# An attention and Mamba kernel whose small TensorE work is handed out at about one matmul a block

## The chip, the cores and the metric

The kernel runs on one core of one Trainium2 chip. The metric is the device time of one execution in microseconds (us). The engines are TensorE (PE, with its weight loads PEld), VectorE (DVE), ScalarE (ACT), GpSimd (POOL) and SyncE (SP), which issues most DMAs.

## The reference

Two layers act on x of shape (4, 128, 64, 64), all in fp32. Layer 0 is self-attention over the 4096 pixels of each image, with 4 heads of 32 channels, followed by a residual and a layer norm over channels. Layer 1 is the sum of three branches on the result: a 3x3 convolution, a spectral branch (a 2-D FFT, a 1x1 product over real and imaginary parts, the inverse FFT), and a Mamba block. Cut to what matters:

```python
attn = softmax(q @ k.T * scale); y = layernorm(attn @ v @ Wo + bo + x) * gamma + beta   # layer 0
spatial = conv3x3(y, conv_spatial_w) + conv_spatial_b
spectral = irfft2(conv1x1(rfft2(y)))
xi, z = split(u @ in_proj_w.T)                      # u: y as (pixels, 128); 256 channels each
xs = silu(conv1d_causal(xi, 4 taps))
dt = softplus(xs @ x_proj -> 8 -> dt_proj + b);  B, C = xs @ x_proj -> 16 + 16
h[t] = exp(dt[t] * A) * h[t-1] + dt[t] * B[t] * xs[t]     # 256 channels x 16 states
ym = ((sum over states of h * C) + xs * D) * silu(z) @ out_proj_w.T
out = spatial + spectral + ym
```

## The kernel before

**Blocks.** An image is cut into 8 chunks of 512 pixels; there are 32 chunks. Attention handles a chunk in two units, one per pair of heads (H = 0 to 63), each against all 4096 keys. The program is one long Python loop over *blocks* (`u`), and every engine executes its instructions in the order in which this loop records them. One unit takes 16 blocks, one chunk 32 (`SLOT`). A block during attention holds, on PE in this order:

- `scores_for_max` (L444), four matmuls into a two-bank PSUM tile (tag sA) for a coming unit; DVE takes the row maxima of it (L451);
- two times `scores_for_exp` (L486), six matmuls each, the first into tag sB, the second into tag sC; ACT takes exp of each (L494);
- a second `scores_for_max` with its L451, again in sA, of which there is one buffer;
- other PE work, see below;
- two times `times_values` (L506), exp times V into tag o.

The eight PSUM banks are sA, sB and sC with two each, m and o with one each.

**The scan.** 64 blocks (`LAG = 2 * SLOT`) behind attention, each block also does one of a chunk's 32 scan steps (16 states, two halves of channels): ACT writes the decay exp(dt A) to PSUM in one half of a tile with tag sC (`scan_decay`, L771), DVE runs the scan (`scan_state`, L784), POOL multiplies with C (L788) and adds to the sum (L803), and prepares dt B xs two steps ahead (`scan_input_term`, L776). For the last two chunks PE sums instead (L797), and after attention has ended DVE does L776.

**Other work.** Everything else is a set of generators that `Plan` drives: K and V projections (`project_kv`, L365 and L378), queries (`project_q`, L423), the transposes of maxima (`maxima`, L457, L466, L473), the output projection with layer norm (L562, L563, bn_stats L571, L589), the inputs of the Mamba block (`mamba_input` L639, `scan_input` L663 with the causal taps L670/L675 on DVE), `scan_bc` (L696), `scan_dt` (L707 to L737), `gate` (L746), `spectral` (L813, L820, L821), `convolve` (nine matmuls L840 and one L844) and `scan_output` (L894). A generator yields a string of what its next step needs: P a place for a matmul, C one of the convolution, T a temporary PSUM bank, A a place on ACT, D, E and g on DVE at three points of the block, M the lasting bank, x and f buffers. Each block has so many places of each kind, and the jobs take them by rank and by due time (`plan.at(u, rank, job)`). The temporaries of a block are the two banks of one tile `tmp` with tag sB, made when the first is asked for:

```python
t = psum.tile([P, 2, L], F32, tag="sB", name=f"tmp_{u}")
return [t[:, 0, :], t[:, 1, :]]
...
places = {"P": 2, "C": 1, "T": 2, "A": 3, "D": 2, "E": 1, "G": 1}
```

`sigmoid` is built of exp and ln, since one table set holds both: Abs, Exp and Ln(1 + .) on ACT, one DVE instruction at point g, after the scan (L611), which reads the logarithm, and Exp again (L613). The logarithm (L609) takes a temporary bank of its own. Each chunk has four sigmoids, two of the taps' output and two of the gate. `scan_dt` has a logarithm of the same kind, twice a chunk (L724, read by L727).

Of the kernel before, what the change touches and what calls it, by code (L numbers as in the profile page):

```python
# [9 lines left out]
F32 = mybir.dt.float32  # L10
# [7 lines left out]
P = 128  # L18
# [5 lines left out]
L = 512  # L24
# [57 lines left out]
class Job:  # L82
# [3 lines left out]

    def __init__(self, gen, u):  # L90
        self.gen = gen
        self.done = False
# [11 lines left out]
class Plan:  # L104


    def __init__(self, temporary, lasting, buffers):
        self.u = None
        self.places = {}
        self.buffers = buffers  # L110
        self.temporary, self.lasting = temporary, lasting
        self.seq = 0
        self.later = []
        self.jobs = []
        self.freed = []
# [11 lines left out]

    def begin(self, u, places):
        self.u = u
        self.places = dict(places)  # L130
        self.temps = []
        self.buffers["M"] += sum(when <= u for when in self.freed)
        self.freed = [when for when in self.freed if when > u]

    def phase(self, kinds):
        u = self.u
        for e in sorted((e for e in self.later if e[0] <= u), key=lambda e: e[:3]):
            self.jobs.append((e[1], e[0], e[2], Job(e[3], u - 1)))
            self.later.remove(e)
        self.jobs = sorted((j for j in self.jobs if not j[3].done), key=lambda j: j[:3])  # L140
        for *_, job in self.jobs:
            while not job.done and self.may(job, kinds):
                bank = None
                for c in job.need:
                    if c == "T":
                        if not self.temps:
                            self.temps = self.temporary(u)
                        bank = self.temps.pop(0)
                    elif c == "M":
                        bank = self.lasting(u)  # L150
                    if c in self.buffers:
                        self.buffers[c] -= 1
                    elif c != "g":
                        self.places[c] -= 1
                job.advance(bank, u)
        self.jobs = [j for j in self.jobs if not j[3].done]
# [14 lines left out]
def attention_then_conv_mamba(  # L171
# [19 lines left out]
    B, C, N = x.shape  # L191
# [144 lines left out]
    rows = [slice(j * HS, (j + 1) * HS) for j in range(2)]  # L336
    used = [slice(j * HS, j * HS + HD + 1) for j in range(2)]

    def temporary(u):

        t = psum.tile([P, 2, L], F32, tag="sB", name=f"tmp_{u}")
        return [t[:, 0, :], t[:, 1, :]]

    def lasting(u):
        return psum.tile([P, L], F32, tag="m", name=f"sum_{u}")

    plan = Plan(temporary, lasting, {"x": 2, "f": 1, "M": 1})


    def load_x(c, tag, bufs):  # L350
# [250 lines left out]
    def sigmoid(z, tag, nm):  # L601

        a = loc.tile([P, L], F32, tag=tag, name=f"sg_{nm}", bufs=1)
        yield "A"
        nc.scalar.activation(a, z, AF.Abs)
        yield "A"
        nc.scalar.activation(a, a, AF.Exp, scale=-1.0)
        ln = yield "ATG"
        nc.scalar.activation(ln, a, AF.Ln, bias=ones)  # L609
        yield "g"  # L610
        nc.vector.scalar_tensor_tensor(a, z, 0.0, ln, ALU.min, ALU.subtract)  # L611
        yield "A"
        nc.scalar.activation(a, a, AF.Exp)  # L613
        return a
# [90 lines left out]
    def scan_dt(c, hf, xd):  # L705
        pdt = yield "PTA"
        nc.tensor.matmul(  # L707
            pdt, dtw[:, hf * P : (hf + 1) * P], xd[:DTR, :], start=True, stop=True
        )


        z = loc.tile([P, L], F32, tag=f"dt{hf}", name=f"dt_{c}_{hf}")
        nc.scalar.activation(z, pdt, AF.Identity, bias=col("dt_b", hf))
        e = loc.tile([P, L], F32, tag=f"sg{hf}", name=f"spe_{c}_{hf}", bufs=1)
        yield "A"
        nc.scalar.activation(e, z, AF.Abs)
        yield "A"
        nc.scalar.activation(e, e, AF.Exp, scale=-1.0)
        yield "A"
        u = loc.tile([P, L], F32, tag=f"u{hf}", name=f"u_{c}_{hf}")  # L720
        w = u
        nc.scalar.activation(w, e, AF.Identity, bias=ones)
        ln = yield "AATG"
        nc.scalar.activation(ln, w, AF.Ln)  # L724
        nc.scalar.activation(w, w, AF.Identity, bias=minus_one)
        yield "g"
        nc.vector.scalar_tensor_tensor(z, z, 0.0, ln, ALU.max, ALU.add)  # L727
        nc.gpsimd.tensor_tensor(e, w, e, ALU.subtract)
        nc.gpsimd.tensor_tensor(z, z, e, ALU.subtract)
        nc.gpsimd.tensor_tensor(u, z, xss[c][hf], ALU.mult)  # L730
        dts[c][hf] = z
        us[c][hf] = u

        for _ in range(2):
            yield ""
        yield "A"
        nc.scalar.activation(xss[c][hf], xss[c][hf], AF.Copy, scale=col("D", hf))  # L737
        scaled.add((c, hf))
# [23 lines left out]
    def scan_decay(c, v):  # L762
        n, hf = divmod(v, NH)
        k = hf * NS + n


        if plan.u > UNITS and v % 2:
            dA[c, v] = psum.tile([P, L], F32, tag="o", name=f"dA_{c}_{k}")
        else:
            dA[c, v] = psum.tile([P, 2, L], F32, tag="sC", name=f"dA_{c}_{k}")[:, 0, :]  # L770
        nc.scalar.activation(dA[c, v], dts[c][hf], AF.Exp, scale=negA[:, k : k + 1])  # L771

    def scan_input_term(c, v, engine):
# [55 lines left out]
    def convolve(c):  # L829

        i = c % NCH
        while c not in edges or c not in hxs:
            yield ""
        flat = yield "PMC"
        pf = flat.rearrange("p (r w) -> p r w", w=W)
        for k in range(9):
            if k:
                yield "PC"
            dy, dx = divmod(k, 3)
            nc.tensor.matmul(  # L840
                pf, cw[:, k, :], xps[c][:, dy : dy + RPC, dx : dx + W], start=k == 0, stop=False
            )
        yield "PCA"
        nc.tensor.matmul(flat, g_hil, hxs.pop(c), start=False, stop=True)  # L844
        plan.release()
        ym = loc.tile([P, L], F32, tag="ym", name=f"ym_{c}", bufs=2)
        yms[c] = ym
        nc.scalar.activation(ym, flat, AF.Identity, bias=col("conv_b"))
        if i == 0:
            nc.gpsimd.tensor_tensor(ym[:, :W], ym[:, :W], sbias, ALU.add)  # L850
# [20 lines left out]
    def scan_output(c):  # L871

        b, i = divmod(c, NCH)
        late = i < NCH // 2
        yield "f"
        while not all(gates[c]):
            yield ""

        for hf in range(NH):
            if c >= CHUNKS - 2:  # L880
                acc = loc.tile([P, L], F32, tag=f"acc{hf}", name=f"acc_{c}_{hf}")
                nc.vector.tensor_tensor(acc, accs[c, hf], gates[c][hf], ALU.mult)
                accs[c, hf] = acc
            else:
                nc.gpsimd.tensor_tensor(accs[c, hf], accs[c, hf], gates[c][hf], ALU.mult)
        if not late:
            wr = load_flipped(c)
        yield ""
        yield ""
        while c not in yms:  # L890
            yield ""
        pf = yield "PPTE"
        for hf in range(NH):
            nc.tensor.matmul(  # L894
                pf, outw[:, hf, :], accs[c, hf], start=hf == 0, stop=hf == NH - 1
            )
        ob = loc.tile([P, L], F32, tag="ob", name=f"ob_{c}", bufs=1)
        nc.vector.tensor_tensor(ob, yms.pop(c), pf, ALU.add)
        if late:
            yield ""  # L900
            ymd[c] = dram.tile([P, L], F32, tag="ymd", name=f"ymd_{c}", bufs=NCH)
            nc.sync.dma_start(ymd[c], ob)
        else:
            add_flipped(ob, wr)
            yield ""
            yield ""
            nc.sync.dma_start(out[b, :, i * L : (i + 1) * L], ob)
        plan.buffers["f"] += 1
# [22 lines left out]
    UH = NT // 2  # L931
    SLOT = PAIRS * UH
    UNITS = HALVES * UH
    LAG = 2 * SLOT
    STATES = NH * NS
    for b in range(B):


        u0 = (b * NCH - 1) * SLOT + 2
        for i in range(NCH):  # L940
            plan.at((b - 1) * NCH * SLOT + i * SLOT + 20 if b else 3 - SLOT + i, 0, project_kv(b, i))
            for k in range(PAIRS):
                plan.at(u0 + k * UH + 2 * i, 0, place_k(b, k, i))
            plan.at(u0 + UH + 2 * i, 0, place_v(b, i))
# [8 lines left out]
    for c in range(CHUNKS):  # L953
# [2 lines left out]
        plan.at(u0 + 8, 1, mamba_input(c))  # L956
        plan.at(u0 + SLOT + 19, 3, convolve(c))
        plan.at(c * SLOT + LAG + 5, 3, gate(c))
        plan.at((c + 1) * SLOT + LAG, 0, scan_output(c))
    for b in range(B):  # L960
        for i in range(NCH // 2):
            plan.at((b + 1) * NCH * SLOT + 22 + 5 * i, 4, flips(b * NCH + NCH // 2 - 1 - i))
# [4 lines left out]

            scores_for_max(h + 1, s, "sC" if h < 0 and s % 2 else "sA")

    places = {"P": 2, "C": 1, "T": 2, "A": 3, "D": 2, "E": 1, "G": 1}  # L970
    most = {"P": 4, "C": 4, "T": 2, "A": 4, "D": 4, "E": 4, "G": 4}
    u = 3 - SLOT
    end = (CHUNKS + 3) * SLOT
    while u < end or not plan.idle():
# [14 lines left out]
        n = v // NH + 2  # L989
        if v % NH == 0 and 0 <= n < CHUNKS * NS:  # L990
            scan_load(*divmod(n, NS))
        plan.phase(["P", "C", "T", "A", "E", "G", "M", "x", "f", ""])
        if scan:
            scan_state(*divmod(v, STATES))
        if 0 <= v + 2 < CHUNKS * STATES:
# [83 lines left out]
```

## Time and profile before

| | |
|---|---|
| median of 3 runs | 6483.5 us (6479.47 to 6487.86) |
| the profiled execution's own time | 6482.18 us |
| its span, first to last instruction | 6480.4 us |
| granted clock of TensorE, mean | 0.983 |
| busy: PE, DVE, ACT, POOL | 5923.2, 4457.2, 3688.8, 4632.6 us |
| last attention block ends at about | 6211 us |

A line such as `L451 DVE TENSOR_REDUCE part<-s` names the source line, the engine, the operation, what is written and what is read. "A <- B" in the table of waits means that A stood idle until B was done. Matmul busy times overlap each other, since matmuls are pipelined.

### The profile page before, as it was taken

The numbers are of one execution on the slowest core, as the hardware profiler recorded it, in microseconds if no ns is written. First come the engines' busy times: TensorE is split into PE (matmuls) and PEld (weight loads), VectorE is DVE, ScalarE is ACT, GpSimd is POOL, SyncE is SP. The second block draws the span as 40 slices with busy tenths as digits, with TensorE's granted clock in tenths as the row PEclk, the third lists the DMA queues.
The fourth block names the chain that finished last, engine by engine and source line by source line (L and its number), as shares of the span: only waits on it lengthen the run. The fifth ranks groups of instructions, "written<-read, shape, count | busy, mean of one in ns | idle before, by whom it ended". The sixth has DMA issues, their size and how long they took to land.

```text
span 6480.4 us, 84221 instructions
## 1 busy us (share of the span) xinstructions
PE 5923.2 (91%) x32076; PEld 2624.0 (40%) x32076; DVE 4457.2 (69%) x4396; ACT 3688.8 (57%) x4922; POOL 4632.6 (71%) x4960
## 2 busy tenths in 40 slices
PE   5999999999999999999999999999999999999976
PEld 2444444444444444444444444444444444444421
DVE  3557777677776777777777777767777777777645
ACT  1456565566555656556556656555655665666642
POOL 0017777777787777777787777777778777777866
PEclk8999999999999999999999999999999999999976
DMA  3002222223222222222322221222322222212223
GB/s 107 14 26 56 60 54 61 60 61 90 71 71 61 61 61 53 60 58 71 89 78 63 58 61 53 61 60 63 89 66 70 56 56 56 50 52 56 58 61 88
DMA packets 234229, 405.01 MB, mean 62 GB/s; under 512 B 38872, under 2 KB 40416, under 8 KB 233824
## 3 DMA queue, kind: packets, MB, share of 16 engines
q1 hardware_dynamic: 229440, 397.75, 23.8%
q8 instruction: 251, 4.11, 0.3%
q10 hardware_dynamic: 4384, 1.89, 0.1%
q14 instruction: 154, 1.26, 0.1%
HBM read 350.54 MB, written 49.02 MB: 62 GB/s over the span
## 4 chain that ended last, share of the span: by engine, by line
PE 65%; ACT 14%; DVE 9%; POOL 4%; issue 4%; DMA 3%; SPq 0%; ACTq 0%; POOLq 0%; DVEq 0%
PE po L506 21%; PE s L486 15%; PE s L444 15%; ACT e L494 7%; DVE part L451 4%; PE sum L840 4%; ACT dA L771 3%; POOL hs L788 2%; DMA xk<-in_x 2%; DVE hs L784 2%; DVE xh L589 1%; PE tmp L562 1%; PE tmp L707 1%; ACT tmp L609 1%; PE tmp L894 1%
## 5 line engine op out<-in xcount | busy, mean ns | idle before, releaser
L451 DVE TENSOR_REDUCE part<-s 128x2 f32<-128x1024 f32 x2048 | 2502.0, 1223 | 1455.3 <-PE s L444 1450.3
L494 ACT ACTIVATE e<-s 128x1024 f32<-128x1024 f32 x2048 | 1986.9, 1022 | 2217.2 <-PE s L486 2217.2
L506 PE MATMUL po<-e,V 128*33 128x512 f32 x8192 | 1986.6, 599 | 1.4 <-ACT e L494 1.2
L444 PE MATMUL s<-K,Q 64*128 64x512 f32 x8192 | 1501.0, 445 | 101.7 <-DVE part L451 95.9
L784 DVE TENSOR_TENSOR_SCAN hs<-dA,state,db 128x512 f32<-128x512 f32 x1024 | 1310.8, 1280 | 279.4 <-ACT dA L771 220.5
L486 PE MATMUL s<-Q,K 64*128 64x512 f32 x8192 | 1302.1, 395 | 171.8 <-DVE sg_x L611 92.3
L788 POOL TENSOR_TENSOR hs<-hs,bc 128x512 f32<-128x512 f32 x1024 | 1313.7, 1283 | 81.9
L776 POOL TENSOR_TENSOR db<-u,bc 128x512 f32<-128x512 f32 x963 | 1231.4, 1279 | 0.0
L803 POOL TENSOR_TENSOR acc<-acc,hs 128x512 f32<-128x512 f32 x900 | 1154.8, 1283 | 70.6
L444 PEld LDWEIGHTS s<-K,Q 64*128 64x128 f32 x8192 | 621.5, 186 | 1320.1 <-DVE part L451 811.4
L787 POOL COPY state<-hs 128x1 f32<-128x1 f32 x1024 | 216.2, 211 | 1022.4 <-DVE hs L784 1019.5
L486 PEld LDWEIGHTS s<-Q,K 64*128 64x128 f32 x8192 | 750.8, 184 | 428.4 <-DVE sg_x L611 113.6
L506 PEld LDWEIGHTS po<-e,V 128*33 128x33 f32 x8192 | 389.4, 109 | 1194.4 <-issue 594.3
L486 PE MATMUL s<-MX,sel 64*128 64x512 f32 x4096 | 807.6, 390 | 0.0
L771 ACT ACTIVATE dA<-dt,negA 128x512 f32<-128x512 f32 x1024 | 707.5, 691 | 126.5 <-DVE hs L784 95.1
L486 PEld LDWEIGHTS s<-MX,sel 64*128 64x128 f32 x4096 | 385.3, 184 | 88.1
L840 PE MATMUL sum<-xp,cw 128*128 128x512 f32 x576 | 318.6, 638 | 0.0
L797 PE MATMUL acc<-hs,cst 128*128 128x512 f32 x128 | 112.7, 988 | 89.5 <-POOL hs L788 89.4
L460 POOL COPY wide<-mx 128x128 f32<-128x128 f32 x256 | 63.7, 295 | 154.9 <-DVE mx L457 90.2
L685 POOL TENSOR_TENSOR xs<-xs,sg_x 128x512 f32<-128x512 f32 x64 | 82.1, 1282 | 111.2 <-ACT sg_x L613 111.2
L840 PEld LDWEIGHTS sum<-xp,cw 128*128 128x128 f32 x576 | 91.9, 192 | 129.7 <-issue 129.7
L538 POOL TENSOR_TENSOR oz<-oz,rz 128x512 f32<-128x512 f32 x64 | 81.3, 1270 | 87.4 <-DMA rz<-rd 79.5
(189 smaller groups left out, 3652.4 us busy)
## 6 DMA issues: line engine op xcount, KB each, us to landing
bc<-bcd SPq DMA_DIRECT2D x512, 512.0 KB
K<-kd SPq DMA_DIRECT2D x64, 256.0 KB
rz<-rd SPq DMA_DIRECT2D x128, 128.0 KB
vd<-vst SPq DMA_DIRECT2D x32, 264.0 KB
V<-vd SPq DMA_DIRECT2D x32, 264.0 KB
xq<-in_x SPq DMA_DIRECT2D x32, 256.0 KB
xk<-in_x SPq DMA_DIRECT2D x32, 256.0 KB
kd<-khi SPq DMA_DIRECT2D x32, 256.0 KB
```

The costliest lines, as they stand in the source:

```text
L444: nc.tensor.matmul(sc[:, j, :], QT[H][rows[j], n, t * P : (t + 1) * P], KK[k][m][rows[j], :], start=n == 0, stop=n == 1,)
L451: nc.vector.tensor_reduce(part[H][:, t, :, m], sc, AX.X, ALU.max)
L486: nc.tensor.matmul(s[:, j, :], sel[rows[j], :] if n == 2 else KK[k][i][rows[j], t * P : (t + 1) * P], mov[rows[j], :], start=n == 0, stop= ...
L494: nc.scalar.activation(e, s, AF.Exp)
L506: nc.tensor.matmul(po[H][used[j], :], VA[i][:, t, 2 * k + j, :], e[:, j, :], start=m == 0, stop=m == NT - 1,)
L771: nc.scalar.activation(dA[c, v], dts[c][hf], AF.Exp, scale=negA[:, k : k + 1])
L776: engine.tensor_tensor(db[c, v], us[c][hf], bcs[c, n][:, 0, :], ALU.mult)
L784: nc.vector.tensor_tensor_scan(hs, dA.pop((c, v)), db.pop((c, v)), state[:, k : k + 1], ALU.mult, ALU.add)
L787: nc.gpsimd.tensor_copy(state[:, k : k + 1], hs[:, L - 1 :])
L788: nc.gpsimd.tensor_tensor(hs, hs, bcs[c, n][:, 1, :], ALU.mult)
L803: nc.gpsimd.tensor_tensor(accs[c, hf], accs[c, hf], hs, ALU.add)
L840: nc.tensor.matmul(pf, cw[:, k, :], xps[c][:, dy : dy + RPC, dx : dx + W], start=k == 0, stop=False)
```

## The change

Four things are changed in the code.

1. *Places.* P falls from 2 to 1.2 a block, and what is left over (up to 1) is carried into the next block. A job that needs more P than there is sets one aside for the next block. The kind C is dropped, so the convolution competes for P alone.
2. *Temporaries.* There is one T a block, the first bank of a tile `first` with tag sB (outside attention there may be two). The logarithms of `sigmoid` and `scan_dt` ask for the new kind U instead of T: the second bank of a tile `second` with tag sC, whose first bank holds the block's decay.
3. *Times and ranks.* `LAG` is 8 blocks more; K and V projections of later images may start 24 blocks earlier and have rank 2 instead of 0; `scan_output` has rank 2 instead of 0.
4. *scan_output* asks for the buffer f after its products with the gate instead of before them.

```diff
@@ class Plan
-    def __init__(self, temporary, lasting, buffers):
+    def __init__(self, banks, buffers):
...
+        self.kept = 0
...
     def begin(self, u, places):
         self.u = u
+        left = self.places.get("P", 0) + self.kept
+        self.kept = 0
         self.places = dict(places)
-        self.temps = []
+        self.places["P"] += min(left, 1)
...
         for *_, job in self.jobs:
+            if "P" in kinds and job.need.count("P") > self.places["P"]:
+                self.places["P"] -= 1
+                self.kept += 1
             while not job.done and self.may(job, kinds):
                 bank = None
                 for c in job.need:
-                    if c == "T":
-                        if not self.temps:
-                            self.temps = self.temporary(u)
-                        bank = self.temps.pop(0)
-                    elif c == "M":
-                        bank = self.lasting(u)
+                    if c in self.banks:
+                        bank = self.banks[c](u)
@@ temporaries
     def temporary(u):
-        t = psum.tile([P, 2, L], F32, tag="sB", name=f"tmp_{u}")
-        return [t[:, 0, :], t[:, 1, :]]
+        if u not in first:
+            first[u] = [psum.tile([P, 2, L], F32, tag="sB", name=f"first_{u}"), 0]
+        first[u][1] += 1
+        return first[u][0][:, first[u][1] - 1, :]
+
+    def banks_of_second(u):
+        if u not in second:
+            second[u] = psum.tile([P, 2, L], F32, tag="sC", name=f"second_{u}")
+        return second[u]
+
+    def beside_decay(u):
+        return banks_of_second(u)[:, 1, :]
...
-    plan = Plan(temporary, lasting, {"x": 2, "f": 1, "M": 1})
+    plan = Plan({"T": temporary, "U": beside_decay, "M": lasting}, {"x": 2, "f": 1, "M": 1})
@@ sigmoid
-        ln = yield "ATG"
+        ln = yield "AUG"
@@ scan_dt
-        ln = yield "AATG"
+        ln = yield "AAUG"
@@ scan_decay
-            dA[c, v] = psum.tile([P, 2, L], F32, tag="sC", name=f"dA_{c}_{k}")[:, 0, :]
+            dA[c, v] = banks_of_second(plan.u)[:, 0, :]
@@ convolve
-        flat = yield "PMC"
+        flat = yield "PM"
...
-                yield "PC"
+                yield "P"
...
-        yield "PCA"
+        yield "PA"
@@ scan_output
-        yield "f"
         while not all(gates[c]):
             yield ""
...
+        yield "f"
         if not late:
             wr = load_flipped(c)
@@ times, ranks, places
-    LAG = 2 * SLOT
+    LAG = 2 * SLOT + 8
...
-            plan.at((b - 1) * NCH * SLOT + i * SLOT + 20 if b else 3 - SLOT + i, 0, project_kv(b, i))
+            plan.at((b - 1) * NCH * SLOT + i * SLOT - 4 if b else 3 - SLOT + i, 2 if b else 0, project_kv(b, i))
...
-        plan.at((c + 1) * SLOT + LAG, 0, scan_output(c))
+        plan.at((c + 1) * SLOT + LAG, 2, scan_output(c))
...
-    places = {"P": 2, "C": 1, "T": 2, "A": 3, "D": 2, "E": 1, "G": 1}
-    most = {"P": 4, "C": 4, "T": 2, "A": 4, "D": 4, "E": 4, "G": 4}
+    places = {"P": 1.2, "T": 1, "U": 1, "A": 3, "D": 2, "E": 1, "G": 1}
+    most = {"P": 4, "T": 2, "U": 1, "A": 4, "D": 4, "E": 4, "G": 4}
...
-        plan.phase(["P", "C", "T", "A", "E", "G", "M", "x", "f", ""])
+        plan.phase(["P", "T", "U", "A", "E", "G", "M", "x", "f", ""])
```

## The prediction

> **What bounds the kernel now.** I read the page first: TensorE (PE) is busy 91% of the span, no other engine over 71%. The window view of one chunk in mid-run, of a late chunk and of the tail comes next (columns: length; busy time and count of PE, weight loads, DVE, ACT, POOL; granted clock; DMA share; GB/s).
>
> ```profile
> PE 5923.2 (91%) x32076; PEld 2624.0 (40%) x32076; DVE 4457.2 (69%) x4396; ACT 3688.8 (57%) x4922; POOL 4632.6 (71%) x4960
> ```
>
> ```profile
> 3001.84:3194.46 192.62, 180.27 (x1001) 80.35 (x1000) 137.76 (x136) 115.25 (x154) 148.90 (x159) 1.00 0.35 90
> 5088.97:5278.22 189.25, 177.86 (x990) 79.08 (x988) 136.75 (x135) 114.06 (x153) 149.04 (x159) 1.00 0.21 55
> ...
> 6211.00:6361.80 150.80, 93.38 (x148) 32.39 (x148) 85.85 (x97) 48.92 (x84) 87.25 (x96) 0.67 0.33 79
> 6361.80:6465.00 103.20, 66.35 (x88) 20.64 (x88) 58.46 (x61) 26.45 (x40) 61.15 (x67) 0.67 0.34 89
> ```
>
> A chunk of 32 blocks repeats every 192.62 us (6.02 a block), and PE has about 12 us of gaps in it. Timing each block from its first L444 matmul to the next block's, a block with no other PE work lasts 4.56 us wherever nothing is late, one with one 128x512 matmul pair-pass (L840, L746, L844) 5.62: 1.06 a matmul. All other PE work of a chunk, costed so (21 such pieces 22.3; two output projections 3.06; the L894, L696 and L820/821 products 5.66; three sets of transposes 1.77), makes 32.8 us, so 145.9 + 32.8 = 178.7 us is stall-free and 13.9 us a chunk is stall. The table of waits (engine and line, what it waited for: us in total, times, longest) says of what:
>
> ```profile
> ACT e L494 <- PE s L486: 2217.2, 1030, 12.2
> ...
> PE s L486 <- DVE sg_x L611: 92.3, 62, 2.4
> ...
> PE s L486 <- DVE sg_z L611: 71.6, 60, 1.5
> ...
> PE tmp L663 <- ACT mhi L471: 39.1, 31, 1.4
> ...
> PE tmp L813 <- ACT xi L666: 29.3, 31, 1.1
> ...
> PE tmp L746 <- ACT Q L426: 27.1, 29, 1.0
> ...
> PE tmp L423 <- ACT vst L388: 19.6, 24, 0.8
> ```
>
> ACT's 2217 us of waiting for PE confirms the bound; it costs nothing. PE itself waits in two ways. First, two temporaries in one block share one tile `tmp`: the second matmul waits for ACT to read the first. Second, after a block with the sigmoid's logarithm (L609, in `tmp`), the first exponent scores of the next block (L486, same tag sB) wait for DVE's L611, which reads that logarithm. One block of each, from the timeline (start, length):
>
> ```profile
> 3004.59 1.13 PE L423 MATMUL tmp<-xq,wq_t 128*128 128x512 f32 x2
> ...
> 3005.91 0.67 ACT L426 ACTIVATE Q<-tmp,bq 128x512 fp32r<-128x512 f32 x1
> ...
> 3006.63 1.13 PE L746 MATMUL tmp<-xp,inw 128*128 128x512 f32 x2 [0.92 <-ACT Q L426]
> ```
>
> ```profile
> 3037.74 1.28 DVE L784 TENSOR_TENSOR_SCAN hs<-dA,state,db 128x512 f32<-128x512 f32 x1 [0.18 <-ACT dA L771]
> ...
> 3038.22 0.69 ACT L609 ACTIVATE tmp<-sg_z,ones 128x512 f32<-128x512 f32 x1
> 3038.95 0.69 DVE L611 SCALAR_TENSOR_TENSOR sg_z<-zg,tmp 128x512 f32<-128x512 f32 x1
> ...
> 3039.55 1.22 DVE L451 TENSOR_REDUCE part<-s 128x2 f32<-128x1024 f32 x1
> ...
> 3039.69 0.73 PE L486 MATMUL s<-Q,K 64*128 64x512 f32 x4 [0.90 <-DVE sg_z L611]
> ```
>
> In the second excerpt the scan L784 starts at 3037.74 although the logarithm ends only at 3038.91: the two are in different tiles. And L451 of the next block starts behind L611.
>
> **Two rules of the Trainium skill.** The page "PSUM — Partial Sum Buffer", section "PSUM bank collisions raise a hardware error", asks for guards by bank and quadrant. The two halves of `tmp` are two banks, so L746 would need no guard against a reader of the other half; the 0.92 us row shows that this program guards by tile. I go by the row. The same page's section "Engine vs sequencer instructions" says that the queues of ScalarE, VectorE and GpSimdE are strict FIFO; the rows agree (L451 after L611), so what holds the scan holds everything behind it on DVE.
>
> **The change, part by part.** The order of the changed program, engine by engine, gives each block's contents.
>
> *Pairs in one tile: gone.* With T at one a block, the four pair blocks of a chunk (L466+L663 7.60 us, L663+L813 7.72, L423+L746 7.68, L378+L423 7.60) split. Against 4.56 plus their parts they hold 1.39 + 1.04 + 1.00 + 0.93 = 4.4 us. Saved in full, except that a lone L466 block is short (5.15 us): L473, ending 6.2 after block start, then holds the next L486 (due at 5.72): 0.5 us, and 0.2 for the other one, which starts late itself.
>
> *Logarithms beside the decay: a new wait.* They leave sB, so L486 into sB is free. But decay and logarithm are now halves of one tile, decay written first, logarithm second, and scan_state read after both. By the tile guard the scan waits for the logarithm, and in the built program its semaphore count is indeed the logarithm's. Queued behind the scan on DVE: L611 (or L727), then the next block's two L451, which free sA for PE. The due times in a block: decay ends 4.13, scan 4.24, next thing on DVE 1.17 after the scan's start, L451 0.60 after L611's, due 0.78 into the next block; each us that it is late is a us of block. Six logarithms a chunk:
> - conv1d half 1: two L675 in the block make it 4.69; Abs, Exp, Ln after the decay end at 6.07, scan 6.17, L611 7.34, L451 7.94: 7.94 - 4.69 - 0.78 = 2.47. Half 2, block 4.56: 2.60.
> - gate half 1: only Ln follows the decay (4.82): 4.92, 6.09, 6.69: 1.35. Half 2 stands with L378 and two more ACT steps (6.1) in a block of 6.6: 0.6.
> - dt, two: with a convolution matmul (5.62 or more), Ln ends 5.32: 0.85 and 0.2. In before L727 costs nothing here.
> Sum 8.1. In before the same L611 waits cost 1.69 + 1.05 + 1.62 + 1.62 and 0.5 more with L516 behind one of them: 6.5.
>
> *Blocks without other work* fall from 306 to 182 of 864, with pieces that DVE work used to hide behind. L571/L573 leave a gate block for an empty one: 0.3 + 0.3. L589 (3.18 us for four, slowed by POOL) in an empty block with one L457: 1.9 + 0.3, against 1.65 now beside the L611 wait. The two L516 a chunk (each 0.95: the next L451 is behind it) stay, one of them no longer merged with L611: 1.9 against 0.95 beside the 0.5 above. Small rest 0.3 against 0.6.
>
> Sum after: 8.1 + 0.7 + 0.6 + 2.2 + 1.9 + 0.3 = 13.8 us a chunk, before 14.1 by the same list (13.9 by subtraction). For the eight chunks without K/V projections I get 12.0 against 189.25 - 176.55 = 12.7. So 22 x (-0.25) + 8 x (-0.7) = -11 us, and -5 us for the opening, where pairs and logarithms run without a scan. Main phase: -16 us, with perhaps 0.8 us a chunk of error, 25 us.
>
> *LAG + 8.* Eight more scan blocks run after attention has ended. They belong to chunk 29, whose sums run on POOL: copy, L788, L803 take 0.2 to 0.65 + 1.28 + 1.28, some 3.1 us with gaps; the last 32 blocks of the tail average 3.0 without, the 32 before 4.7 with the last chunk's chain. Bounds 22 to 38; I take 27. Hidden by nothing: the tail is the end.
>
> *Ranks and times of project_kv, scan_output, the f buffer, C:* same instructions and DMAs, earlier or later by blocks; K/V are placed a chunk later and the L365 wait for xk (0.1 to 0.3 us) goes. On SP the xk loads pass bc, which have a block or more in hand; POOL's L885 is now ahead of the wait for f. Nothing, 0 to 5 us either way.
>
> **Sum.** 6482.2 (own time of the profiled execution; span 6480.4; median of the runs 6483.5) - 16 + 27 = 6493; I add 4 for waits that a list by hand misses: 6497.
>
> **Rivals.**
> 1. *The logarithm doesn't hold the scan.* Then L611 costs only its place before L451: 1.3 + 1.4 + 0.7 + 0.3, nothing for dt; 3.7 instead of 8.1, and 30 x -4.4 - 16 + 27: 6360. For it: banks differ. Against: the 0.92 us row and the built count. 5%.
> 2. *The list is right but over-booked*, DVE catching up in long blocks: 0.5 to 1.2 us less a chunk, 6455 to 6480. 30%, part of it no measurable change.
> 3. *POOL becomes the bound (slower).* It is busy 149 of 192.6 us a chunk and starts each block's four operations at the scan's end. If six scans of up to 1.9 us late (8 us idle) can't be made up, acc and the hs buffers come late and the next scan waits. It decides once lateness plus 149 exceeds the chunk where extras bunch, 2 us a chunk: 6555. Two to three db tiles in hand speak against it. 12%.
> 4. *The spreading isn't done.* Excluded: no block of the built order has two temporaries during attention.
>
> **Chances.** A difference of 0.2%, 13 us, is about what a measurement can tell. Forecast as listed (53%): half of it is over 13 us slower. With the rivals: faster 0.16, same 0.30, slower 0.54. Range 6455 to 6540: the main phase's 25 us both ways, the tail's bounds, and part of rivals 2 and 3.
>
> **What would show it.** Right: L663, L813, L746 and L423 have no more PE waits for ACT; DVE's scan waits for the logarithm's line some 1 to 1.9 us, six times a chunk; PE L444 (second maximum) waits for L451 up to 2.6 us after such blocks; a mid-run chunk again 191 to 194 us; 72 scans after attention. Wrong: a chunk under 189 (rival 1), or POOL rows with no idle time and scans waiting for db (rival 3).

## The result: slower, 6554.2 us for a forecast of 6497

The kernel after the change takes 6554.2 us (median of 4 runs, 6552.3 to 6557.6), the kernel before 6483.1; the ratio is 1.011, 95% interval 1.0092 to 1.0127. The forecast had the sign, but the time is 57 us above it and 14 us above the range. The profiled execution took 6553.4 us with a span of 6551.6. Line numbers of after are those of before plus 14: L444 is L458, L486 is L500, the sigmoid's logarithm L609 is L623, its reader L611 is L625, the scan L784 is L798. Most kernels of the experiments shift them by a few more; e5 has those of before.

Busy time of the engines after, from the page:

```profile
PE 6034.2 (92%) x32076; PEld 2665.5 (41%) x32076; DVE 4428.3 (68%) x4404; ACT 3711.2 (57%) x4922; POOL 4621.8 (71%) x4952
```

PE has exactly as many instructions as before (32076), but 111 us more busy time. A slower clock would do that: the clock records of the two traces hold 445 us at half clock in after and 217 in before, and the work of the extra 228 us, done at half clock, takes some 114 us longer (an estimate from these two sums). The window view of after, for a mid-run chunk, a late chunk and the two parts of the tail, with the columns as in the prediction:

```profile
3002.75:3197.00 194.25, 183.93 (x1002) 82.10 (x1002) 136.50 (x135) 115.97 (x154) 148.88 (x159) 0.98 0.33 91
...
5119.80:5310.90 191.10, 181.25 (x990) 80.73 (x988) 135.85 (x134) 114.80 (x152) 148.60 (x158) 0.98 0.20 55
6251.00:6402.00 151.00, 76.37 (x136) 27.86 (x135) 81.01 (x93) 50.40 (x86) 96.86 (x103) 0.70 0.28 73
6402.00:6551.60 149.60, 94.76 (x119) 27.74 (x118) 83.67 (x87) 33.25 (x50) 85.44 (x92) 0.65 0.30 83
```

A mid-run chunk takes 194.25 us for 192.62, a late one 191.10 for 189.25, and the granted clock of both reads 0.98 where it read 1.00. The last `po` (the last product of exp with V, so the end of attention) ends at 6250.9 us for 6209.0 (+41.9), and what follows takes 300.8 us for 271.4 (+29.4). Together that is the 71 us of the result.

The table of waits, PE's part and then the scan's and POOL's:

```profile
PE s L458 <- DVE part L465: 134.0, 320, 1.9
PE s L500 <- DVE sg_x L625: 125.5, 61, 2.8
...
PE s L500 <- DVE sg_z L625: 29.8, 31, 2.2
...
PE first L677 <- ACT e L508: 0.9, 2, 0.4
```

```profile
POOL state L801 <- DVE hs L798: 1117.9, 693, 16.8
...
DVE hs L798 <- ACT second L623: 204.2, 116, 9.6
...
DVE hs L798 <- ACT second L738: 83.6, 60, 7.0
```

The waits of pairs for ACT are gone: of L677 (before L663, 39.1 us) 0.9 is left. The new wait is there too: the scan L798 waits for the sigmoid's logarithm L623, 1.76 us a time, and for that of the time step L738, 1.39. So far it is the forecast. The timeline (start, length) of a block behind the logarithm of conv1d half 1; the block starts on PE with the L458 at 3087.09, of which this row shows the first four matmuls:

```profile
3087.09 0.73 PE L458 MATMUL s<-K,Q 64*128 64x512 f32 x4
...
3087.84 0.69 ACT L623 ACTIVATE second<-sg_x,ones 128x512 f32<-128x512 f32 x1
...
3088.13 0.40 PE L500 MATMUL s<-MX,sel 64*128 64x512 f32 x2
...
3088.63 1.28 DVE L798 TENSOR_TENSOR_SCAN hs<-second,state,db 128x512 f32<-128x512 f32 x1 [1.60 <-ACT second L623]
3089.83 0.66 DVE L625 SCALAR_TENSOR_TENSOR sg_x<-xs,second 128x512 f32<-128x512 f32 x1
...
3090.55 0.73 PE L500 MATMUL s<-Q,K 64*128 64x512 f32 x4 [2.02 <-DVE sg_x L625]
...
3091.68 1.22 PE L458 MATMUL s<-K,Q 64*128 64x512 f32 x4 [0.17 <-DVE part L465]
...
3092.84 2.07 PE L827 MATMUL first<-cst,xh 128*128 128x128 f32 x8
```

Logarithm, scan, L625, then PE: the chain is the one forecast, and the second L458 starts 4.60 us into its block (forecast: 2.06, as in a block where nothing is late, and 2.47). One link differs. The forecast had PE waiting at the second L458 for the row maxima L465; here that wait is 0.17 us, and 2.02 us stand at the second exponent scores L500. They need a tile of the tag sC, where the logarithm now is, until L625 has read it. The sum is the same, since L465 is ready only just before.

But this second L458 takes 1.22 us, while the one at 3087.09 took 0.73. In the trace the granted clock is 0.5 from 3091.65 for 3.41 us. The windows just before and during this stretch, and during the like one three blocks later:

```profile
3088.24:3091.65 3.41, 1.25 (x10) 0.48 (x6) 3.02 (x4) 1.41 (x3) 1.51 (x3) 1.00 0.20 68
3091.65:3095.07 3.42, 3.39 (x14) 2.47 (x16) 3.38 (x4) 2.29 (x4) 3.42 (x3) 0.50 0.58 123
3108.72:3112.13 3.41, 1.32 (x12) 0.57 (x8) 2.71 (x3) 1.59 (x2) 1.29 (x2) 1.00 0.36 105
3112.13:3115.55 3.42, 3.27 (x9) 1.40 (x8) 2.10 (x3) 1.71 (x2) 3.34 (x4) 0.50 0.23 77
```

PE is busy 1.25 and 1.32 us of the first and third window, and the window after each runs at half clock. Between 700 and 6100 us the trace of after has 52 such stretches of 3.41 us, each behind a gap of 2.0 to 2.1 us ahead of L500, in the two blocks of a chunk behind the x logarithms; the trace of before has no stretch there. The page "TensorE: Matmul & The Clock Gate" of the Trainium skill, section "What's actually happening", states the two clocks and a free-running window of 4096 cycles, 3413 ns; the stretches agree with both (0.5 of the full clock, 3.41 us).

### The profile page after: what moved, and what is told of

It reads as the page before. It is cut to its first block, busy times and chain, and to the rows that moved or that the text cites. A ratio compares the mean times of both kernels' runs of the same rounds, so it can differ in the third digit from the quotient of the medians.

```text
span 6551.6 us, 84002 instructions
## 1 busy us (share of the span) xinstructions
PE 6034.2 (92%) x32076; PEld 2665.5 (41%) x32076; DVE 4428.3 (68%) x4404; ACT 3711.2 (57%) x4922; POOL 4621.8 (71%) x4952
## 3 DMA queue, kind: packets, MB, share of 16 engines
q10 hardware_dynamic: 4384, 1.89, 0.1%
q14 instruction: 153, 1.25, 0.1%
## 4 chain that ended last, share of the span: by engine, by line
PE 63%; DVE 17%; ACT 11%; POOL 4%; issue 3%; DMA 1%; ACTq 0%; SPq 0%; DVEq 0%; POOLq 0%
PE po L520 20%; PE s L458 15%; PE s L500 13%; DVE part L465 7%; DVE hs L798 6%; ACT e L508 5%; PE sum L854 3%; ACT second L785 2%; POOL hs L802 2%; PE first L437 1%; ACT second L623 1%; DVE xh L603 1%; PE first L576 1%; PE first L760 1%; PE first L677 1%
## 5 line engine op out<-in xcount | busy, mean ns | idle before, releaser
L465 DVE TENSOR_REDUCE part<-s 128x2 f32<-128x1024 f32 x2048 | 2502.1, 1223 | 1431.8 <-PE s L458 1425.8
L458 PE MATMUL s<-K,Q 64*128 64x512 f32 x8192 | 1517.3, 449 | 139.8 <-DVE part L465 134.0
L798 DVE TENSOR_TENSOR_SCAN hs<-second,state,db 128x512 f32<-128x512 f32 x988 | 1264.3, 1280 | 465.6 <-ACT second L623 204.2
L500 PE MATMUL s<-Q,K 64*128 64x512 f32 x8192 | 1318.9, 400 | 189.6 <-DVE sg_x L625 125.5
L790 POOL TENSOR_TENSOR db<-u,bc 128x512 f32<-128x512 f32 x955 | 1216.1, 1273 | 0.0
L458 PEld LDWEIGHTS s<-K,Q 64*128 64x128 f32 x8192 | 625.1, 187 | 1378.1 <-DVE part L465 734.4
L500 PEld LDWEIGHTS s<-Q,K 64*128 64x128 f32 x8192 | 745.4, 185 | 479.7 <-DVE sg_x L625 146.1
L500 PE MATMUL s<-MX,sel 64*128 64x512 f32 x4096 | 811.6, 392 | 0.0
L785 ACT ACTIVATE second<-dt,negA 128x512 f32<-128x512 f32 x988 | 683.3, 692 | 92.4 <-DVE hs L798 58.1
L500 PEld LDWEIGHTS s<-MX,sel 64*128 64x128 f32 x4096 | 387.8, 185 | 88.9
```

Of the source, the lines that this page charges most:

```text
L458: nc.tensor.matmul(sc[:, j, :], QT[H][rows[j], n, t * P : (t + 1) * P], KK[k][m][rows[j], :], start=n == 0, stop=n == 1,)
L465: nc.vector.tensor_reduce(part[H][:, t, :, m], sc, AX.X, ALU.max)
L500: nc.tensor.matmul(s[:, j, :], sel[rows[j], :] if n == 2 else KK[k][i][rows[j], t * P : (t + 1) * P], mov[rows[j], :], start=n == 0, stop= ...
L790: engine.tensor_tensor(db[c, v], us[c][hf], bcs[c, n][:, 0, :], ALU.mult)
L798: nc.vector.tensor_tensor_scan(hs, dA.pop((c, v)), db.pop((c, v)), state[:, k : k + 1], ALU.mult, ALU.add)
```

## The experiments

Theory after this reading: the waits are as forecast, and the clock that falls behind them is what the forecast lacks. Rivals: POOL or the waits themselves take the time, or contention, or the spreading of PE's work.

**e1_warm: keep PE busy in the gap.** The repeats overwrite the same scores.

```diff
@@ scores_for_exp
-        for n, mov in enumerate((QT[H][:, 0, :], QT[H][:, 1, :], MX[H])):
+        once = (QT[H][:, 0, :], QT[H][:, 1, :], MX[H])
+        again = 3 if tag == "sB" and plan.u in behind else 1
+        for n, mov in list(enumerate(once)) * again:
...
@@ sigmoid
         ln = yield "AUG"
+        if "_x" in nm:
+            behind.add(plan.u + 1)
```

> The changed kernel, but in each block behind one of the two logarithms of the taps' sigmoid, PE computes the six score matmuls into sB three times over instead of once (the same values into the same bank), so that about 1.4 us of the 2.2 us gap ahead of the scores into sC is filled. Nothing else waits for less. Theory (late scores into sC leave PE idle 2.2 us, and the granted clock then falls to a half for 3.41 us, twice a chunk, at 1.2 to 1.6 us each): the half-clock stretches in mid-run go, 30 x 2.8 = 84 us at most, so about 6480 us (6465 to 6500). Rival (the slower matmuls cost nothing beyond the wait, the whole loss is the wait): 6545 to 6560.

Measured: 6473.5 us, ratio to before 0.998 (0.9972 to 0.9988). With 744 matmuls more, it is 81 us faster than after. First a chunk of it; then the window that holds the first of the two gaps, with the one behind it; then the scan's waits for the logarithms:

```profile
2953.90:3145.10 191.20, 183.62 (x1024) 82.49 (x1022) 136.44 (x136) 115.93 (x154) 148.96 (x159) 1.00 0.33 94
```

```profile
3052.64:3056.06 3.42, 2.62 (x21) 1.38 (x18) 3.42 (x4) 1.64 (x2) 2.03 (x3) 1.00 0.17 57
3056.06:3059.47 3.41, 3.41 (x22) 1.65 (x20) 3.25 (x4) 2.23 (x4) 3.25 (x4) 1.00 0.47 147
```

```profile
DVE hs L802 <- ACT second L627: 201.0, 115, 9.6
...
DVE hs L802 <- ACT second L742: 82.8, 59, 7.0
```

PE is busy 2.62 us there, the next window stays at 1.00, and a chunk is 3 us shorter. Three mid-run stretches are left. The scan waits as long as in after (201.0 for 204.2 us, 82.8 for 83.6), and POOL is as busy (4627.5 us), so neither the scan's waits nor POOL's work makes the 81 us; nor does contention, as PE has more work here than in after. The clock theory holds. The two blocks behind the x logarithms, 9.69 and 10.50 us in after, are 8.18 and 9.08 here; the list of the prediction gives 5.62 + 2.47 = 8.1 and 6.68 + 2.60 = 9.3.

**e2_logs_sbuf: the logarithms in SBUF.**

```diff
-        ln = yield "AUG"
+        yield "AG"
+        ln = att.tile([P, L], F32, tag="ln", name=f"ln_{nm}", bufs=1)
@@ scan_dt: likewise, "AAUG" becomes "AAG"
```

> The changed kernel, but the six logarithms of a chunk are written to a tile in SBUF (one buffer) instead of the bank beside the decay; they need no U. Theory (the scan is held only because decay and logarithm share a tile): scans start with the decay again, L611 and L727 only take their place ahead of the next L451; the six cost 3.7 us a chunk instead of 10.9 measured, no half clock in mid-run, a chunk of about 187 us, 6554 - 30 x 7.2 = 6338 us. Rival 1 (two SBUF operands make L611 and L727 wait for POOL, up to 0.6 us each): 6338 + 30 x 3.6 = 6446. Rival 2 (thinly spread PE work itself is what costs): above 6483.

Measured: 6461.3 us, ratio 0.9957 (0.9943 to 0.9971): a miss by 123 us. The scan no longer waits for the logarithm, but DVE's L626, which now reads both operands from SBUF, does worse. Its timeline in the same block:

```profile
3054.97 0.72 ACT L624 ACTIVATE ln_x<-sg_x,ones 128x512 f32<-128x512 f32 x1
...
3055.68 1.28 POOL L804 TENSOR_TENSOR hs<-hs,bc 128x512 f32<-128x512 f32 x1
3055.73 1.78 DVE L626 SCALAR_TENSOR_TENSOR sg_x<-xs,ln_x 128x512 f32<-128x512 f32 x1 [0.38 <-ACT ln_x L624]
...
3057.43 1.21 DVE L465 TENSOR_REDUCE part<-s 128x2 f32<-128x1024 f32 x1
...
3058.70 0.90 PE L458 MATMUL s<-K,Q 64*128 64x512 f32 x4 [2.33 <-DVE part L465]
```

L626 takes 1.78 us (in after 0.66). It starts 0.05 us behind POOL's L804 and ends 0.55 us after it, as an instruction does that waits for the other to finish: the Trainium skill's page "SBUF — State Buffer", section "SBUF: two separate sides", says that a DVE operation with two SBUF inputs and a GpSimd one that reads SBUF exclude each other for a whole instruction. The rows agree: of the 64 such L626 behind x logarithms 62 start while a POOL operation runs and end about 0.55 us after it, and the other two take 0.69 us. This is the cause that rival 1 named. That its 6446 us is near is luck in part, as it has no half clock in it. So the gap is not gone but has moved to the second L458, 2.33 us long, and 51 half-clock stretches are there again.

**e3_logs_in_first: the logarithms in the second bank of `first`,** apart from the decay.

```diff
     def beside_decay(u):
-        return banks_of_second(u)[:, 1, :]
+        if u not in first:
+            first[u] = [psum.tile([P, 2, L], F32, tag="sB", name=f"first_{u}"), 0]
+        return first[u][0][:, 1, :]
```

> The changed kernel, but the logarithms go to the second bank of the tile `first` (tag sB), as they did before the change; places, LAG and ranks stay as changed. Theory: the scores into sB wait for L611 again (1.0 to 1.7 us, four times a chunk, about 5.0 in all instead of 10.9), the scan doesn't, no half clock in mid-run: 6554 - 30 x 5.9 = 6377 us. Rival (spreading costs by itself): 6483 or more.

Measured: 6354.8 us, ratio 0.9799 (0.9784 to 0.9813). It beats both kernels. A chunk of it:

```profile
2900.47:3087.65 187.18, 179.71 (x1001) 80.55 (x999) 137.46 (x136) 115.06 (x154) 149.01 (x159) 1.00 0.36 96
```

187.18 us at full clock: 7.1 below after. About 3 of them are the clock (by e1); the other 4, by subtraction, are what the logarithm costs more beside the decay than in `first`. The scan waits for no logarithm here, but the exponent scores into sB wait for its reader (L627) again, as in before:

```profile
PE s L502 <- DVE sg_x L627: 94.5, 62, 2.4
...
PE s L502 <- DVE sg_z L627: 27.8, 31, 1.8
```

**e4_before_beside: in the kernel before, only the logarithms put beside the decay.**

```diff
@@ sigmoid; scan_dt likewise
-        ln = yield "ATG"
+        yield "AUG"
+        ln = banks_of_second(plan.u)[:, 1, :]
...
@@ scan_decay
-            dA[c, v] = psum.tile([P, 2, L], F32, tag="sC", name=f"dA_{c}_{k}")[:, 0, :]
+            dA[c, v] = banks_of_second(plan.u)[:, 0, :]
...
```

> The kernel before, with one part of the change alone: the logarithms beside the decay in a tile of tag sC (one U a block); two P, two T, LAG 64, all ranks as before. Theory: the pairs in one tile still cost 4.4 us a chunk, the six logarithms 11.5 instead of 6.5, and the clock falls after three of them, some 3 to 4 us: 30 x 8.5 more, 6740 us (6640 to 6760). Rival (beside the decay is no dearer than in sB, the loss comes from the spreading): 6470 to 6500.

Measured: 6870.3 us, ratio 1.0591 (1.0575 to 1.0607); right in direction, 130 us above. Its trace has 101 half-clock stretches in mid-run, 26 of them double; the expectation had not counted on so many.

From the traces so far I took the length of a gap for the cause: PE gaps up to 1.8 us were hardly ever followed by half clock, those from 2.0 us mostly.

**e6_warm_little: fill only a little of the gap.**

```diff
-        for n, mov in enumerate((QT[H][:, 0, :], QT[H][:, 1, :], MX[H])):
+        once = (QT[H][:, 0, :], QT[H][:, 1, :], MX[H])
+        again = 1 if tag == "sB" and plan.u in behind else 0
+        for n, mov in [(3, once[0])] * again + list(enumerate(once)):
...
```

> After, with two more score matmuls (the first two of the second exponent scores, computed once more and overwritten) in the block behind an x logarithm, so that the idle gap of PE there falls from about 2.05 to about 1.75 us. Over the traces so far no gap up to 1.8 us in otherwise busy stretches was followed by half clock, and nearly all from 2.0 on were. Theory: the length of one gap decides, and the step lies between 1.8 and 2.0 us; then the half-clock stretches are gone as in e1_warm and the time is 6474 (6465 to 6485). Rival: it is the busy share of a longer stretch; then a part of the stretches stays and the time is 6500 to 6555.

Measured: 6559.8 us, ratio 1.0116 (1.01 to 1.0131): no gain over after, with 55 stretches; it misses the 6474 of the theory and lies some 5 us above the 6500 to 6555 of the rival, by which some stretches were to go. The gap did shrink, to between 1.8 and 1.9 us, so the rule by gap length is wrong. The gap, and the windows around it:

```profile
3092.58 0.73 PE L502 MATMUL s<-Q,K 64*128 64x512 f32 x4 [1.80 <-DVE sg_x L629]
```

```profile
3091.23:3094.65 3.42, 1.89 (x12) 1.05 (x13) 3.38 (x5) 1.65 (x3) 2.48 (x3) 1.00 0.01 4
3094.65:3098.06 3.41, 3.41 (x14) 1.85 (x15) 2.84 (x3) 1.92 (x3) 3.15 (x5) 0.50 0.78 157
```

So I counted windows instead. In each trace the half-clock stretches start on one grid: start modulo 3413.3 ns agrees within 10 ns from the 5th to the 95th percentile. For each window of that grid between 700 and 6050 us that is not itself at half clock, I took the share in which a matmul ran, and whether the next window is at half clock. The eleven changed kernels together, those below included:

| share of the window in which PE is busy | windows | next one at half clock |
|---|---|---|
| under 0.42 | 211 | 211 |
| 0.42 to 0.5 | 79 | 60 |
| 0.5 to 0.6 | 408 | 60 |
| 0.6 and more | 16172 | 9 |

The window above has 1.89 of 3.42 us, 0.55: in the mixed zone. So have e3's two windows behind its x logarithms (1.94 and 1.85 us in the chunk looked at), though in e3 only one of 55 such windows was followed by half clock. e3 is near the edge as well.

**e5_before_lag8: in the kernel before, `LAG = 2 * SLOT + 8` and nothing else.**

> The kernel before with LAG eight blocks more and nothing else. Theory (the tail step of the prediction, +27, and 29.4 us more after the last po in the trace of after): the eight scan blocks left over after attention are the whole of it, attention ends where it ended (6209 us within 5), and the time is 6510 (6505 to 6518). Rival: the longer tail comes from the later rank of scan_output and the later request for f, not from LAG; then this kernel stays at 6480 to 6495.

Measured: 6540.1 us, ratio 1.0089 (1.0072 to 1.0105): a miss by 30 us. The tail is 298.0 us for 271.4, +26.6 as the theory says; but attention ends at 6236.1, 27 later. A mid-run chunk grew by about 2 us, a late one shrank by about 1.4. The scan blocks now meet the attention blocks at another offset, and one job of POOL comes late for it, as PE's waits show:

```profile
PE tmp L466 <- POOL wide L460: 34.0, 20, 1.7
```

In before this wait is 0 (L466 waited for nothing but 0.5 us for ACT). Of the 18 half-clock stretches in mid-run 14 stand behind it. Another of them falls behind an x logarithm, in the same place where before keeps its clock. The window there and the next one of e5, and then the like window of before:

```profile
3088.57:3091.98 3.41, 1.91 (x14) 1.16 (x14) 3.01 (x5) 2.09 (x4) 1.85 (x3) 1.00 0.00 0
3091.98:3095.39 3.41, 3.41 (x12) 1.58 (x9) 3.37 (x4) 3.24 (x4) 2.13 (x2) 0.50 0.59 139
```

```profile
3070.62:3074.03 3.41, 1.94 (x16) 1.15 (x14) 3.02 (x4) 2.10 (x4) 2.25 (x3) 1.00 0.00 0
```

After 1.91 us of work the clock falls, after 1.94 it doesn't: both lie in the mixed zone of the table, so the kernel before was near the edge without showing it. So the tail's term holds, but "LAG alone" was not a change of the tail alone.

**e8_e4_warm: e4 with e1's repeats behind every logarithm.**

> e4_before_beside, with the six second-score matmuls before the gap computed three times in the block behind each logarithm. e4_before_beside has 127 times 3.41 us at half clock in mid-run (26 of its 101 stretches are double), and 81 us for 52 in after is 1.56 each. Theory: what went beyond the forecast for e4_before_beside (6870 for 6740) is the clock; the stretches behind x logarithms (74 of 127 lots) go, those behind other gaps may stay: 6755 (6710 to 6790). Rival: the excess lies in blocks that hold a pair of temporaries and are late for other reasons; then 6830 to 6870.

Measured: 6744.0 us, ratio 1.0402 (1.0386 to 1.0417): 126 us less than e4, within the range expected, and about as much as e4's excess of 130. 30 stretches are left, 23 of them behind another gap of 2.6 us.

**e7_first_lag66: e3 with `LAG = 2 * SLOT + 2`.**

> e3_logs_in_first with LAG six blocks less (66 instead of 72). Theory: each block of LAG costs the tail 29.4 / 8 = 3.7 us, and the main phase doesn't need the eight blocks; 6355 - 22 = 6333 (6326 to 6340). Rival: with fewer blocks between the time step and its first use, decays and scans of a chunk's start come late in the main phase; then 6345 or more.

Measured: 6351.9 us, ratio 0.9795 (0.9781 to 0.981): only 3 us less than e3, a miss by 19 and in the rival's range. An early chunk, a mid-run chunk and the tail of it:

```profile
1040.25:1231.32 191.07, 182.44 (x1001) 81.68 (x1000) 137.22 (x136) 114.89 (x154) 147.44 (x157) 0.98 0.25 59
2740.72:2927.85 187.13, 179.82 (x1000) 80.46 (x999) 137.27 (x135) 114.95 (x154) 147.32 (x157) 1.00 0.25 60
6077.91:6353.00 275.09, 170.18 (x251) 55.48 (x250) 155.68 (x168) 79.39 (x130) 164.03 (x177) 0.67 0.30 80
```

The tail is 23.7 us shorter than e3's 298.8, as expected. Six early chunks lose it, 3.9 us each: there the planner orders the jobs otherwise, a time-step matmul (L723) stands where it waits 2.1 us for ACT's L740, which writes the same tile, and the clock falls behind that, and once more 15 blocks earlier.

**e9_first_lag68: e3 with `LAG = 2 * SLOT + 4`,** which keeps e3's order of blocks.

> e3_logs_in_first with LAG four blocks less (68 instead of 72). Unlike with 66, every chunk in mid-run has the block contents of e3_logs_in_first, but for one gate matmul that stands in a block with a wait of 1.7 us instead of in a long one. Theory: in e7_first_lag66 the tail did give 23.7 us back, and the order of its first nine chunks, 4 us slower each and with half clock, took them again; with 68 the tail gives 4 x 3.7 = 15 and the main phase is as in e3_logs_in_first or better: 6340 (6325 to 6345). Rival: the main phase is slower with any smaller LAG, since the time step is nearer to its first use: 6355 or more.

Measured: 6346.8 us, ratio 0.9785 (0.977 to 0.9799), the lowest time of all, but 2 us above the range expected. The tail gives 10.6 us back where 15 were expected, and attention ends 9 later than in e3's trace. The intervals of the two ratios overlap, so whether e9 is better than e3 isn't settled.

**e10_sbuf_warm: e2 with the exponent scores of tag sC computed twice** in the block behind an x logarithm.

> e2_logs_sbuf, with the six second-score matmuls of tag sC computed twice in the block behind an x logarithm, where PE otherwise idles 2.3 us for the second maximum. e2_logs_sbuf has 51 half-clock stretches in mid-run, all in these two blocks of a chunk. Theory (clock): at 1.5 us each, 6461 - 78 = 6383 (6370 to 6400), and what then remains above 6338 is L626 with both operands in SBUF, 1.64 us at the x halves where the one of after takes 0.66: 2 x 0.98 x 30 = 59 less what overlaps. Rival: PE waits for the second maximum anyway, so that the clock costs nothing there: 6440 to 6460. For the windows of 3.413 us on the grid of the half clocks, both new runs should repeat the count of the nine before: under 0.5 busy, more than 9 in 10 are followed by half clock; at 0.6 or more, none.

Measured: 6406.3 us, ratio 0.9877 (0.9861 to 0.9894): 55 us less than e2, between theory and rival. The windows with the two gaps and those behind them:

```profile
3026.55:3029.96 3.41, 1.77 (x14) 1.06 (x11) 3.38 (x5) 2.27 (x3) 3.33 (x4) 1.00 0.55 104
3029.96:3033.37 3.41, 3.41 (x12) 0.91 (x10) 2.35 (x3) 0.69 (x1) 1.89 (x3) 0.50 0.14 50
...
3047.03:3050.44 3.41, 1.92 (x12) 0.88 (x9) 2.58 (x3) 2.00 (x3) 3.33 (x4) 1.00 0.33 97
3050.44:3053.85 3.41, 3.41 (x14) 0.94 (x14) 2.52 (x3) 1.20 (x2) 2.61 (x4) 1.00 0.00 0
```

A share of 0.52 fell, one of 0.56 didn't. 11 stretches are left where e2 had 51, and all 11 follow windows between 0.5 and 0.6, a zone for which the expectation had said nothing. Its count for the rest: of this run's and e9's windows 5 of 6 under 0.5 were followed by half clock (expected: more than 9 in 10, which six windows can't test), and none of 3013 at 0.6 or more (expected: none).

## Why the prediction was wrong, point by point

- **Main phase -16 us: this step failed.** Attention ends 41.9 us later. The term that the sum lacks is the clock behind the waits: it counts each wait by its length and puts the slower matmuls behind it at nothing. With the clock kept (e1), attention ends at 6170.7 us, 38 us earlier than in before; in after it ends 80 us later than in e1, with 54 half-clock stretches more up to there, some 1.5 us each. So the main phase is -38 + 80 where -16 was forecast; without the clock the forecast would have been too high.
- **Stall of 13.8 us a chunk: nearly right for the waits.** With the clock kept (e1) a chunk is 191.20 us, 12.5 above the stall-free 178.7, so the list was 1.3 too high. That is about rival 2's case (0.5 to 1.2 less a chunk), and e1's 6473.5 us lies in its 6455 to 6480.
- **Pairs, 4.4 us a chunk.** Their waits are gone from the table. The saving is not measured alone: a chunk of e3, with the logarithms back in sB, takes 5.4 us less than one of before, but its order of jobs is another too, and the wait for sg_z fell from 71.6 to 27.8 us in the whole run.
- **Six logarithms, 8.1 for 6.5.** The price of the waits was right where it was looked at: the two x blocks, 2.47 and 2.60 of it, come out in e1 within 0.2 us. What it lacks is the clock. The comparison with the old place was mis-sized too: by the list the new place costs 1.6 us a chunk more, while e1 against e3 measures 4.0, or 119 us in all. In the spread order the old place in sB was the cheaper one: PE waits 122 us for L627 in e3, and 164 us for L611 in before.
- **LAG + 8, +27: right.** +29.4 in after, +26.6 in e5's tail; 72 scans start after attention where 64 did. What LAG does to the main phase was not in the forecast: in before another 27 us (e5); in after it was not measured alone.
- **Rival 1** (the logarithm doesn't hold the scan, 6360) didn't occur: the scan is held. e3 measured 6354.8 with the scan free, but its scores into sB wait for L627, which rival 1 has not, so that the two numbers agree is no test of that arithmetic. e3 keeps the spreading, the ranks and LAG and is 130 us faster than before. So the loss comes from where the logarithm stands, and from the tail, and not from the spreading; what places, ranks and times are worth one by one was not measured.
- **Rival 3** (POOL, 6555) named nearly the time measured, with the wrong cause. POOL waits for the scan 1118 us (before 1020), but e1 is 81 us faster with the same POOL work. A time that fits doesn't show its mechanism.

Left open: what the chip counts within a window exactly. The ends of matmuls are modelled in the profile, which may be why shares between 0.42 and 0.6 go either way; 9 stretches follow busier windows. Windows that begin and end 0.2 us earlier part the cases better: one bound at 1.75 us of work then puts 51 of some 16 870 windows on the wrong side, where the windows of the table put 79. That shift was chosen afterwards, so it is a hint only, that the clock changes a little after its window. The limit of about half holds for these kernels and this way of counting.

## What to carry to other kernels

In these kernels a new wait on PE cost its length only while PE stayed busy enough around it. Look at the busy share of the few microseconds around the gap, and add the half-clock time behind it. More busy time for the same instruction count, or a mean granted clock of 0.98 in a stage that had 1.00, points to it. Before putting two values into one tile to save space, ask who reads each: here the neighbour's reader was the scan, and moving the logarithm to a bank of another tile, with nothing else changed, was worth 3% of the time (6554.2 to 6354.8 us).

## What was not expected of the hardware

The clock falls for a pause of 2.0 us in an engine that is 92% busy: 3.41 us at half clock follow, on a fixed grid, when PE was busy under about half of the window before. The Trainium skill's page "TensorE: Matmul & The Clock Gate", section "HAM oscillation — how this bites in real kernels", gives as its rule no PE-idle gaps over about 3.4 us; here gaps of 2.0 us were enough, as 1.25 us of work in a window did not keep the clock, and the measurement decides. Also, useless matmuls in the gap made a kernel 81 us faster.
